# Four-layer graph network on one core: layer 2's nodes transposed by VectorE and transfers, with the surrounding products in a new order

## The chip, the cores and the metric

One core of one Trainium2 chip runs the whole kernel in one launch. The metric is the device time in microseconds (us). The kernel before took 3103.06 us, the median of three runs (3100.27 to 3104.02). Its profile below was taken on a further execution of 3099.01 us, with a span of 3097.3 us and a mean granted TensorE clock of 0.996.

Engines are named as the profile names them: PE is TensorE, PEld its weight load, DVE VectorE, ACT ScalarE, POOL GpSimd, SP SyncE (here only an issuer of transfers).

## The reference, cut to what matters

A batch of 128 graphs with 128 nodes and 256 features passes through four layers. Each is a graph layer with a residual and a layer norm. All is float32.

```python
x = _layernorm(x + L0(x))                       # attention over 512 edges
x = _layernorm(x + L1(x))                       # relu((A*A) @ x @ W1), relu((A*A) @ . @ W2), (A*A) @ . @ W3
# --- layer 2 ---
adj_0 = jnp.diag(jnp.diagonal(adj)); adj_1 = jnp.triu(adj, k=1); adj_2 = jnp.tril(adj, k=-1)
h = jnp.einsum('bjf,kfo->kbjo', x, W)           # W: 3 x 256 x 256
out = adj_0 @ h[0] + adj_1 @ h[1] + adj_2 @ h[2] + bias
x = _layernorm(x + out)
x = _layernorm(x + L3(x))                       # two products with batch norms over all rows
```

What matters here is layer 2. Its product contracts over the 256 features, so TensorE needs x with features on the partitions. Layer 1 leaves it with nodes on the partitions, so every batch element must be transposed.

## The kernel before

Four batch elements make a quad; there are 32. `iteration(k)` works on several quads at once in a software pipeline: layer 3's first product of quad a, the end of layer 1 and then layer 2 of quad c, layer 0 and the start of layer 1 of quad b = c + 1, and the scores and softmax of quads further ahead. The program order is fixed by hand; each engine runs its own instructions in that order.

Products are done in blocks with seven multiplications in place of eight (`Seven`). Three banks, y, z and x, collect them. A step that writes into y again must wait until ScalarE has copied the partial sum out (`part`):

```python
class Seven:
    def p1(self):  self.y = ps("y"); self.mm(self.y, "A11", "B11", True);  self.k1 = self.part(self.y, 0)
    def p5(self):  self.z = ps("z"); self.mm(self.z, "S1", "T1", True)
    def p2(self):  x = ps("x");      self.mm(x, "A12", "B21", True);       self.out(0, 0, x, self.k1)
    def p6(self):  self.mm(self.y, "S2", "T2", False); self.k2 = self.part(self.y, 1)
    def p7(self):  self.mm(self.y, "S3", "T3", False); self.k3 = self.part(self.y, 2); self.out(1, 1, self.z, self.k3)
    def p4(self):  self.mm(self.y, "A22", "T4", False); self.out(1, 0, self.y, None)
    def p3(self):  self.mm(self.z, "S4", "B22", False); self.out(0, 1, self.z, self.k2)
```

S1 to S4 are sums of blocks of the nodes, made by VectorE (`sums_a`). In layer 1's first product (`first_seven`, called w) `part` is a ScalarE copy, and `out` a VectorE sum followed by a ScalarE relu:

```python
def part(bank, i):
    to = room[2 + i % 2]
    nc.scalar.copy(to, bank)
    return to
def out(row, col, bank, kept_):
    h1 = temp("h1")
    if kept_ is not None:
        nc.vector.tensor_add(h1, bank, kept_)
    nc.scalar.activation(h1, bank if kept_ is None else h1, AF.Relu)
```

The third product of layer 1 and its norm, for a pair of batch elements (j = 0 or 2):

```python
def third_mix(k, j):
    po = ps("po1")
    nc.tensor.matmul(po, wt_t, s.s3[j], start=True, stop=True)
    nc.vector.tensor_add(xj, xj, po.rearrange("p (b d) -> p b d", d=D))
    s.mv = norm_stats(wk, xj)                       # two statistics, two aggregations
def third_norm(k, j):
    norm_apply(wk, xj, s.mv, norm_root(wk, s.mv))   # ScalarE root; VectorE reciprocal and scaling
    nc.gpsimd.tensor_add(s.xb[:, j:j + 2, :], xj, bias...)
```

Layer 2 works on two pairs, p = 0 and 1, each with a `Seven` (u and v). Before the first one the nodes are transposed by TensorE into PSUM and copied by ScalarE:

```python
def head(p):
    pt = ps("pt3").rearrange("p (t c n) -> p t c n", t=2, c=DC)
    for t in range(2):
        for c in range(DC):
            nc.tensor.transpose(pt[:, t, c, :], s.xr[:, 2 * p + t, c * P:(c + 1) * P], ident)
    xt = temp("x2t").rearrange("p (t c n) -> p t c n", t=2, c=DC)
    nc.scalar.copy(xt, pt)
    return xt
...
run(u.p1, u.p2, u.p5, u.p6, v.p1, v.p2, u.p7, v.p5, v.p6, u.p4, u.p3, v.p7)
```

`mix(p)` then multiplies by the triangles of the adjacency matrix, `norm` and `normed` do the layer norm. `second(k, between)` is layer 1's second product: 14 block products of 8 matmul records each; `between[i]` hangs other work, such as the rest of layer 2 and the scores of the attention (`score`, three passes of VectorE over 128x1024), behind block product i. A different quad's transposed inputs (`load_turned`, `turn`) are already made by transfers of 32x32 blocks and VectorE's transpose.

Of the kernel before, what the change touches and what calls it, by code (L numbers as in the profile page):

```python
# [8 lines left out]
F32 = mybir.dt.float32  # L9
# [17 lines left out]
def gnn_stack(ctx: ExitStack, tc: tile.TileContext, x, adj, w_qv_t, a, w_out_t, src, dst,  # L27
# [14 lines left out]
    nc = tc.nc  # L42
# [3 lines left out]
    P = 128  # L46
# [18 lines left out]
    def ps(name):  # L65
        return psum.tile([P, 512], F32, tag="ps", name=name)
# [62 lines left out]
    with ExitStack() as phase:  # L129
# [5 lines left out]
        class Seven:  # L135
# [8 lines left out]
            def __init__(self, mm, part, out):  # L144
                self.mm, self.part, self.out = mm, part, out

            def p1(self):
                self.y = ps("y")
                self.mm(self.y, "A11", "B11", True)
                self.k1 = self.part(self.y, 0)  # L150

            def p5(self):
                self.z = ps("z")
                self.mm(self.z, "S1", "T1", True)

            def p2(self):
                x = ps("x")
                self.mm(x, "A12", "B21", True)
                self.out(0, 0, x, self.k1)

# [290 lines left out]
        def adc_tile():  # L451
            return wk.tile([P, R * N], F32, tag="adc", name="adc", bufs=1)
# [120 lines left out]
        def late_sums(k):  # L573
            m2 = [quads[k].m2[:, t].rearrange("p c b n -> p c (b n)") for t in range(7)]
            nc.vector.tensor_sub(m2[T2], m2[B22], m2[T1])
            nc.vector.tensor_sub(m2[T4], m2[B21], m2[T2])

        def second_sums():

# [120 lines left out]
        def third_norm(k, j):  # L700
# [4 lines left out]
                s.xb = wk.tile([P, QB, D], F32, tag="xb", name=f"xb{k}", bufs=1)  # L705
            nc.gpsimd.tensor_add(s.xb[:, j:j + 2, :], xj, bias.unsqueeze(1).to_broadcast([P, 2, D]))  # L706

        def layer2(k, b, room=None):

            s = quads[k]
            adc = adc_tile()
            g = [wk.tile([P, 2, 3 * D], F32, tag="ms", name="g", bufs=1) if room is None else room,
                 adc[:, :6 * D].rearrange("p (t f) -> p t f", t=2)]
            sums = [adc[:, 6 * D:], None]
            half = 3 * D // 2

            def head(p):
# [7 lines that stand above are left out]
                return xt  # L727

            def products(p, xt):
                room = sums[p] if p == 0 else temp("x2s")  # L730
# [3 lines left out]
                sums_a(a, a)  # L734
                keep = {}

                def mm(bank, i, j, new):
                    nc.tensor.matmul(bank[:, :half], a[i], layer2.blocks[j], start=new, stop=True,  # L738
                                     skip_group_check=True)

                def part(bank, i):
                    if i < 2:
# [12 lines left out]
                return Seven(mm, part, out)  # L755
# [20 lines left out]
            x0 = head(0)  # L776
            yield
            u = products(0, x0)
            if b is not None:

                pm = {i: mix2(b, i) for i in (2, 0, 1)}
                x1 = head(1)
                mixed(b, 0, pm[0])
                mixed(b, 1, pm[1])
                pm[3] = mix2(b, 3)
            else:
                x1 = head(1)
            v = products(1, x1)
            if b is not None:
                mixed(b, 2, pm[2])  # L790
                mixed(b, 3, pm[3])
            run(u.p1, u.p2, u.p5, u.p6, v.p1, v.p2, u.p7, v.p5, v.p6, u.p4, u.p3, v.p7)
            pos = [ps("po2").rearrange("p (t d) -> p t d", d=D) for _ in range(2)]
            yield
            scaled(0)
            v.p4()
            yield
            v.p3()
            po = mix(0)
            scaled(1)  # L800
            yield
            mv = norm(0, po)
            yield
            po = mix(1)
            yield
            normed(0, mv)
            mv = norm(1, po)
            yield
            normed(1, mv)
# [113 lines left out]
        def iteration(k):  # L923
            a, c, b, e, g = k - 1, k, k + 1, k + 2, k + 3
            has_c, has_b, has_e, has_g = c < NQ, b < NQ, e < NQ, g < NQ
            if has_b and b > 2:
                quads[b].xr = load_x(b)
            if has_c:
                late_sums(c)
            parts = quads[a].layer2  # L930
            if not has_c:

# [17 lines left out]
            steps = softmax_parts(e) if has_e else iter(())  # L950
            if has_c:
                between = {i: [] for i in range(14)}
                for i in (0, 1, 2, 3, 5, 7):
                    between[i].append(lambda: next(parts, None))
                between[11].append(lambda: next(steps, None))
                if has_g:
                    between[9].append(lambda: turn(g))
                    between[11].append(lambda: query_sums(g))
                for i in (12, 13):
                    between[i].append(lambda: next(steps, None))  # L960
                if has_e:
                    for c_, i in enumerate((0, 2, 4)):
                        between[i].append(lambda c_=c_: score(e, c_ + 1))
                if has_b:
                    for j, i in enumerate((5, 8, 9, 10)):
                        between[i].append(lambda j=j: by_row(b, j))
                second(c, between)
# [56 lines left out]
                pass  # L1024
            if has_e:
                attention(e)
                scatter(e)
            rest = third(c, 2)
            mix1(b, 0)
            mix1(b, 2)  # L1030
            third_mix(c, 0)
            next(rest)
            w = first_seven(b)
# [12 lines left out]
            w.p3()  # L1046
            quads[c].layer2 = layer2(c, b)
            next(quads[c].layer2)
            third_norm(c, 2)
            next(quads[c].layer2)  # L1050

        def iteration_0():

            late_sums(0)
# [28 lines left out]
            mix1(1, 0)  # L1083
            next(rest)
            mix1(1, 2)
            w = first_seven(1)
            next(rest)
            w.p1()
            for _ in steps:
                pass  # L1090
            run(w.p5, w.p2)
            next(rest, None)
            attention(2)
            scatter(2)
            w.p6()
            score(3, 0)
            gather_last(3)
            w.p7()
            third_mix(0, 2)
            w.p4()  # L1100
            w.p3()
            quads[0].layer2 = layer2(0, 1)
            next(quads[0].layer2)
            third_norm(0, 2)
            next(quads[0].layer2)

        def late_loads():
            nc.sync.dma_start(w3_sb, w3.rearrange("(c p) f -> p c f", p=P))
# [562 lines left out]
```

## Time and profile before

| Part of the profile | Value |
|---|---|
| Span | 3097.3 us |
| Instructions | 39721 |
| TensorE clock granted, mean | 0.996 |
| Transposes of layer 2 on PE (L724) | 256, 273 ns each as recorded |
| Copies of them on ACT (L726) | 64, 578 ns median |
| Transposes by VectorE of xg (L336) | 56, 685 ns median |
| Data moved | 340.06 MB, mean 110 GB/s |
| Packets | 220962, of them 132704 under 512 bytes |

The busy time of an engine is an average over stages and does not by itself say what sets the end. PE records overlap, since a matmul is recorded with its whole passage: of two that follow each other, the distance of their starts is the time that PE is held. A float32 matmul appears as two records. An idle time shown in brackets names the instruction that ended the wait. Idle time of an engine counts only where PE, directly or through others, has to wait for that engine.

### The profile page before, as it was taken

How to read it: one execution, taken by the hardware profiler on the slowest of the kernel's cores; microseconds unless marked ns; L12 is line 12 of the kernel's file. 1: busy time of each engine (PE TensorE's matmuls, PEld its weight loads, DVE VectorE, ACT ScalarE, POOL GpSimd, SP SyncE). 2: the span in 40 equal slices, each digit the busy share in tenths (PEclk: the TensorE clock that was granted, in tenths of full speed). 3: DMA queues.
4: the chain of work that ended last, by engine and by line, in shares of the span. 5: the costliest groups of instructions: out<-in, count | busy, mean ns of one | idle time of the engine just before them, and what ended most of it. 6: DMA issues, size and time to landing. Idle time of an engine off the chain costs nothing. (4 is left out here: it accounts for less than half of the span.)

```text
span 3097.3 us, 39721 instructions
## 1 busy us (share of the span) xinstructions
PE 3047.4 (98%) x14576; PEld 2382.0 (77%) x14576; DVE 2311.5 (75%) x4599; ACT 1388.0 (45%) x2547; POOL 652.6 (21%) x536
## 2 busy tenths in 40 slices
PE   8899999999999999999999999999999999999987
PEld 4688888888888888888888888888888887864444
DVE  8777777777777777777777777777777776457888
ACT  3344444344444444443344444444443344326668
POOL 3311112222222121122222211111122220001135
PEclk9999999999999999999999999999999999999999
DMA  5633333334333333333344433333343331015567
GB/s 183 162 103 95 77 97 110 103 103 110 110 103 93 99 103 88 84 103 108 98 110 110 110 96 90 109 95 75 98 110 103 103 110 42 21 44 201 172 206 261
DMA packets 220962, 340.06 MB, mean 110 GB/s; under 512 B 132704, under 2 KB 155104, under 8 KB 212448
## 3 DMA queue, kind: packets, MB, share of 16 engines
q0 software_dynamic: 44688, 148.40, 19.6%
q1 hardware_dynamic: 174320, 188.19, 18.5%
q8 instruction: 116, 1.90, 0.2%
q10 hardware_dynamic: 1760, 0.92, 0.1%
q14 instruction: 78, 0.64, 0.1%
HBM read 252.00 MB, written 85.46 MB: 109 GB/s over the span
## 5 line engine op out<-in xcount | busy, mean ns | idle before, releaser
L602 PE MATMUL ph<-m,w 128*128 128x256 f32 x2048 | 473.1, 379 | 0.0
L682 PE MATMUL p<-w,h 128*128 128x256 f32 x2048 | 462.8, 379 | 0.0
L602 PEld LDWEIGHTS ph<-m,w 128*128 128x128 f32 x2048 | 386.8, 190 | 79.9 <-issue 14.8
L682 PEld LDWEIGHTS p<-w,h 128*128 128x128 f32 x2048 | 388.9, 190 | 66.4 <-issue 7.9
L358 POOL DMA_INDIRECT zs<-qd,src_idx x120 | 116.3, 969 | 1330.2 <-DMA qd<-qt 1295.8
L602 PE MATMUL ph<-m,w_s 128*128 128x256 f32 x1536 | 357.7, 379 | 0.4 <-DVE h L614 0.4
L602 PEld LDWEIGHTS ph<-m,w_s 128*128 128x128 f32 x1536 | 291.7, 190 | 53.7 <-issue 14.8
L358 POOL DMA_INDIRECT zs<-qd,dst_idx x120 | 189.6, 1580 | 339.7 <-DMA zs<-qd,src_idx 330.2
L608 ACT COPY u<-ph 128x512 f32<-128x512 f32 x128 | 74.8, 584 | 354.9 <-PE ph L602 354.9
L440 POOL DMA_INDIRECT attd<-at,att_idx x128 | 142.8, 1116 | 342.3 <-DMA attd<-at,att_idx 251.0
L113 ACT ACTIVATE ln_sd<-ln_mv,eps 128x2 f32<-128x2 f32 x192 | 55.9, 291 | 276.4 <-DVE ln_mv L108 276.3
L618 ACT ACTIVATE h<-h 128x512 f32<-128x512 f32 x192 | 121.1, 631 | 87.2 <-DVE h L614 87.2
L390 DVE SCALAR_TENSOR_TENSOR zs<-zs 128x1024 f32<-128x1024 f32 x125 | 151.3, 1210 | 7.7 <-DMA zs<-qd,dst_idx 5.1
L392 DVE TENSOR_TENSOR zs<-zs,a_bc 128x1024 f32<-128x1024 f32 x125 | 153.2, 1225 | 4.3
L393 DVE TENSOR_REDUCE scores<-zs 128x16 f32<-128x1024 f32 x125 | 152.5, 1220 | 4.3
L745 ACT COPY x2k<-y 128x384 f32<-128x384 f32 x192 | 92.0, 479 | 139.5 <-PE y L738 114.2
L106 DVE BATCH_NORM_STATS2 ln_st<-xr 128x6 f32<-128x256 f32 x384 | 144.5, 418 | 6.6
L121 DVE TENSOR_SCALAR xr<-xr,ln_mv,ln_rs 128x256 f32<-128x256 f32 x384 | 142.5, 413 | 7.0
L459 ACT COPY adc<-ad 128x512 f32<-128x512 f32 x125 | 133.0, 1066 | 7.8 <-DMA ad<-attd 7.8
L706 POOL TENSOR_TENSOR xb<-xr,bias 128x512 f32<-128x512 f32 x64 | 99.1, 1548 | 150.8 <-DVE xr L121 143.7
L559 PE MATMUL pm<-wt_t,h 128*128 128x128 f32 x1024 | 126.8, 277 | 0.0
L559 PEld LDWEIGHTS pm<-wt_t,h 128*128 128x128 f32 x1024 | 121.2, 192 | 1.4 <-issue 1.3
(359 smaller groups left out, 5990.7 us busy)
## 6 DMA issues: line engine op xcount, KB each, us to landing
ad<-attd SPq DMA_DIRECT2D x32, 1024.0 KB, 4.8
zd<-z SPq DMA_DIRECT2D x31, 1024.0 KB, 7.5
zl<-zd SPq DMA_DIRECT2D x62, 512.0 KB, 3.7
xr<-in_x_dram SPq DMA_DIRECT2D x32, 512.0 KB, 7.2
x3d<-xr SPq DMA_DIRECT2D x32, 512.0 KB, 2.6
x3l<-x3d SPq DMA_DIRECT2D x32, 512.0 KB, 4.6
out_dram<-x3l POOLq DMA_DIRECT2D x31, 512.0 KB, 5.0
qd<-qt SPq DMA_DIRECT2D x29, 512.0 KB, 2.6
```

Of the source, the lines that this page charges most:

```text
L106: nc.vector.bn_stats(st[:, i, :], r[:, i, :])
L121: nc.vector.tensor_scalar(r[:, i, :], r[:, i, :], mv[:, i, 0:1], rs[:, i:i + 1], op0=ALU.subtract, op1=ALU.mult)
L358: nc.gpsimd.indirect_dma_start(out=s.z[c], out_offset=None, in_=s.qd, in_offset=bass.IndirectOffsetOnAxis(ap=idx[:, c:c + 1], axis=0), com ...
L390: nc.vector.scalar_tensor_tensor(z, z, SLOPE, z, op0=ALU.mult, op1=ALU.max)
L392: nc.vector.tensor_mul(z3, z3, a_bc.unsqueeze(1).to_broadcast([P, QB, D]))
L393: nc.vector.reduce_sum(s.es[:, c, :], z.rearrange("p (r d) -> p r d", d=DH), axis=AX.X)
L440: nc.gpsimd.indirect_dma_start(out=ad, out_offset=bass.IndirectOffsetOnAxis(ap=att_idx[:, c:c + 1], axis=0), in_=s.at[:, c, :], in_offset= ...
L459: (copy or nc.scalar.copy)(s.adc[:, j * H:(j + 1) * H, :], s.ad.rearrange("p (s r) -> p r s", r=R)[:, j * H:(j + 1) * H, :])
L559: nc.tensor.matmul(pm[:, c // 2, c % 2, :], quads[k].h1[i, c], wt_t, start=True, stop=True)
L602: nc.tensor.matmul(bank[g][:, i].rearrange("p b n -> p (b n)"), wa[:, c, f:f + P], s.m2[:, blk_b, c].rearrange("p b n -> p (b n)"), start= ...
L618: nc.scalar.activation(h, h if src_ is None else src_, AF.Relu)
L682: nc.tensor.matmul(p3[:, t * D:(t + 1) * D], s.h2[f // 2][:, f % 2, j + t, :], w3_sb[:, f, :], start=(f == 0), stop=(f == K2 - 1))
```

## The change

The change takes the transposes of layer 2 off TensorE for 31 of the 32 quads. VectorE transposes the 32x32 blocks of two batch elements in one instruction, and 16 transfers within on-chip memory put the blocks in their places; that is done twice a quad. The result is put into two slots (T2 and T4) of the buffer m2, which layer 1's second product of the next quad will fill later. For that, the sums that fill them (`late_sums`) move into `second`. To give the transfers time, the third product of layer 1 is drawn ahead, the block products of layer 1 and layer 2 are interleaved in a new order, v's products move into `second`, the scores move to other places, and the loading of the attention weights (`load_weights`) comes after the first 16 transfers. The last quad keeps the old form.

```diff
+        def nodes_ahead(k, b):
+            s = quads[k]
+            s.g = wk.tile([P, 2, 3 * D], F32, tag="ms", name="g", bufs=1)
+            s.x2 = [quads[b].m2[:, t].rearrange("p c b n -> p (c b n)") for t in (T2, T4)]
+
+        def turn_nodes(k, p, turned):
+            s = quads[k]
+            nc.vector.transpose(turned, s.xr[:, 2 * p:2 * p + 2, :].rearrange("p b d -> p (b d)"))
+            to = s.x2[p].rearrange("p (m n) -> p m n", n=N)
+            from_ = turned.rearrange("p (m i a) -> p m i a", i=P // B, a=B)     # B = 32
+            for i in range(P // B):
+                for j in range(N // B):
+                    nc.sync.dma_start(to[i * B:(i + 1) * B, :, j * B:(j + 1) * B], from_[j * B:(j + 1) * B, :, i, :])
 ... layer2, where there is a next quad b:
+                u.p1()
+                yield
+                u.p2()
+                yield
+                g[1] = adc_tile()[:, :6 * D].rearrange("p (t f) -> p t f", t=2)
+                u.sums()
+                u.p5()
+                pm = {2: mix2(b, 2)}
+                u.p6()
+                pm[0] = mix2(b, 0)
+                pm[1] = mix2(b, 1)
                 mixed(b, 0, pm[0])
                 mixed(b, 1, pm[1])
+                u.p7()
                 pm[3] = mix2(b, 3)
                 mixed(b, 2, pm[2])
+                u.p4()
+                u.p3()
                 mixed(b, 3, pm[3])
 ...
+                yield                    # from here on in second() of the next iteration
+                v.sums(); scaled(0); po = mix(0); v.p1()
+                yield
+                mv = norm(0, po); run(v.p2, v.p5, v.p6)
+                yield
+                v.p7(); normed(0, mv)
+                yield
+                v.p4()
+                yield
+                v.p3(); scaled(1)
+                yield
+                po = mix(1)
+                yield
+                mv = norm(1, po)
+                yield
+                normed(1, mv)
 ... iteration:
-            if has_c:
-                late_sums(c)
-                for i in (0, 1, 2, 3, 5, 7):
+                between[2].append(lambda: late_sums(c, 0))
+                between[4].append(lambda: late_sums(c, 1))
+                for i in (0, 1, 2, 3, 4, 5, 6, 8):
                     between[i].append(lambda: next(parts, None))
-                    for c_, i in enumerate((0, 2, 4)):
+                    for c_, i in enumerate((2, 4, 7)):
                         between[i].append(lambda c_=c_: score(e, c_ + 1))
 ... iteration, after the first mixing products of quad b:
             third_mix(c, 0)
             next(rest)
+            third_norm(c, 0)
+            nodes_ahead(c, b)
+            turn_nodes(c, 0, quads[c].g...)
+            load_weights(e)
             w = first_seven(b)
-            third_norm(c, 0)
-            next(rest)
-            run(w.p1, w.p5, w.p2)
-            next(rest)
             score(g, 0)
             gather_last(g)
+            next(rest)
+            next(rest)
+            w.p1()
+            next(rest, None)
+            w.p5()
+            third_mix(c, 2)
+            w.p2()
+            parts = quads[c].layer2 = layer2(c, b)
             w.p6()
-            next(rest, None)
+            third_norm(c, 2)
+            turn_nodes(c, 1, kept["adc"][:, :512])
+            next(parts)
             w.p7()
-            third_mix(c, 2)
+            next(parts)
             w.p4()
             w.p3()
-            quads[c].layer2 = layer2(c, b)
-            next(quads[c].layer2)
-            third_norm(c, 2)
-            next(quads[c].layer2)
+            next(parts)
```

The first iteration is changed in the same way.

More of the change, by code (lines that the diff above doesn't have):

```diff
@@ L145, in __init__ @@
                 self.mm, self.part, self.out = mm, part, out
+            y = z = x = None
             def p1(self):
-                self.y = ps("y")
+                if self.y is None:
+                    self.y = ps("y")
                 self.mm(self.y, "A11", "B11", True)
@@ L152, in p5 @@
             def p5(self):
-                self.z = ps("z")
+                if self.z is None:
+                    self.z = ps("z")
                 self.mm(self.z, "S1", "T1", True)
             def p2(self):
-                x = ps("x")
+                x = ps("x") if self.x is None else self.x
                 self.mm(x, "A12", "B21", True)
@@ L571, in mixed, with late_sums @@
             nc.vector.tensor_sub(m2[T3], m2[B22], pm[:, 0])
-        def late_sums(k):
+        def late_sums(k, *parts):
             m2 = [quads[k].m2[:, t].rearrange("p c b n -> p c (b n)") for t in range(7)]
-            nc.vector.tensor_sub(m2[T2], m2[B22], m2[T1])
-            nc.vector.tensor_sub(m2[T4], m2[B21], m2[T2])
+            if 0 in parts:
+                nc.vector.tensor_sub(m2[T2], m2[B22], m2[T1])
+            if 1 in parts:
+                nc.vector.tensor_sub(m2[T4], m2[B21], m2[T2])
         def second_sums():
@@ L706, in third_norm @@
             nc.gpsimd.tensor_add(s.xb[:, j:j + 2, :], xj, bias.unsqueeze(1).to_broadcast([P, 2, D]))
+        def nodes_ahead(k, b):
[10 more added lines that the diff above has]
+                    nc.sync.dma_start(to[i * B:(i + 1) * B, :, j * B:(j + 1) * B], from_[j * B:(j + 1) * B, :, i, :])
         def layer2(k, b, room=None):
             s = quads[k]
[L713 to L716, printed above, removed]
+            if b is None:
+                adc = adc_tile()
+                g = [room, adc[:, :6 * D].rearrange("p (t f) -> p t f", t=2)]
+                sums = [adc[:, 6 * D:], None]
+            else:
+                g = [s.g, None]
+                both = wk.tile([P, 2, 512], F32, tag="h2", name="x2s", bufs=4)
+                sums = [both[:, p] for p in range(2)]
             half = 3 * D // 2
@@ L729, in products @@
             def products(p, xt):
-                room = sums[p] if p == 0 else temp("x2s")
+                room = sums[p] if sums[p] is not None else temp("x2s")
                 a = {f"A{t + 1}{c + 1}": xt[:, t, c, :] for t in range(2) for c in range(DC)}
@@ L733, in products @@
                     a[f"S{i + 1}"] = room[:, i * N:(i + 1) * N]
-                sums_a(a, a)
+                if b is None:
+                    sums_a(a, a)
                 keep = {}
@@ L741, in part @@
                 def part(bank, i):
-                    if i < 2:
+                    if i < 2 and i not in keep:
                         keep[i] = temp("x2k")
@@ L753, in out @@
                         nc.vector.tensor_add(to, bank[:, :half], kept_)
-                return Seven(mm, part, out)
+                seven = Seven(mm, part, out)
+                seven.sums, seven.keep = lambda: sums_a(a, a), keep
+                return seven
             def scaled(p):
@@ L774, in normed @@
                 norm_apply(wk, s.xr[:, 2 * p:2 * p + 2, :], mv, norm_root(wk, mv))
[L776 to L781, printed above, removed]
-                x1 = head(1)
+            if b is None:
+                x0 = head(0)
+                yield
+                u = products(0, x0)
+                x1 = head(1)
+                v = products(1, x1)
+                run(u.p1, u.p2, u.p5, u.p6, v.p1, v.p2, u.p7, v.p5, v.p6, u.p4, u.p3, v.p7)
+                pos = [ps("po2").rearrange("p (t d) -> p t d", d=D) for _ in range(2)]
+                yield
+                scaled(0)
+                v.p4()
+                yield
+                v.p3()
+                po = mix(0)
+                scaled(1)
+                yield
+                mv = norm(0, po)
+                yield
+                po = mix(1)
+                yield
+                normed(0, mv)
+                mv = norm(1, po)
+                yield
+                normed(1, mv)
+            else:
+                u, v = (products(p, s.x2[p].rearrange("p (t c n) -> p t c n", t=2, c=DC)) for p in range(2))
+                u.p1()
[9 more added lines that the diff above has]
+                pm[1] = mix2(b, 1)
@@ L783, in layer2 @@
                 mixed(b, 0, pm[0])
                 mixed(b, 1, pm[1])
+                u.p7()
                 pm[3] = mix2(b, 3)
[L786 to L789, printed above, removed]
                 mixed(b, 2, pm[2])
+                u.p4()
+                u.p3()
                 mixed(b, 3, pm[3])
-            run(u.p1, u.p2, u.p5, u.p6, v.p1, v.p2, u.p7, v.p5, v.p6, u.p4, u.p3, v.p7)
-            pos = [ps("po2").rearrange("p (t d) -> p t d", d=D) for _ in range(2)]
@@ L794, in layer2 @@
[L794 to L809, printed above, removed]
+                v.x, po_0 = ps("x"), ps("po2")
+                v.y, v.z, po_1 = ps("y"), ps("z"), ps("po2")
+                pos = [po.rearrange("p (t d) -> p t d", d=D) for po in (po_0, po_1)]
@@ new lines, in layer2 @@
+                for i in range(2):
+                    v.keep[i] = temp("x2k")
+                yield
+                v.sums()
+                scaled(0)
+                po = mix(0)
+                v.p1()
+                yield
+                mv = norm(0, po)
+                run(v.p2, v.p5, v.p6)
+                yield
+                v.p7()
+                normed(0, mv)
+                yield
+                v.p4()
+                yield
+                v.p3()
+                scaled(1)
@@ L810, in layer2 @@
+                yield
+                po = mix(1)
+                yield
+                mv = norm(1, po)
+                yield
+                normed(1, mv)
             nc.sync.dma_start(x3_dram[k], s.xr.rearrange("p b d -> p (b d)"))
@@ L1026, in iteration @@
                 attention(e)
-                scatter(e)
+                scatter(e, False)
             rest = third(c, 2)
@@ L1032, in iteration @@
             next(rest)
+            third_norm(c, 0)
+            nodes_ahead(c, b)
+            turn_nodes(c, 0, quads[c].g.rearrange("p t f -> p (t f)")[:, :512])
+            if has_e:
+                load_weights(e)
             w = first_seven(b)
-            third_norm(c, 0)
-            next(rest)
-            run(w.p1, w.p5, w.p2)
-            next(rest)
             if has_g:
@@ L1040, in iteration @@
                 gather_last(g)
+            next(rest)
[6 more added lines that the diff above has]
+            parts = quads[c].layer2 = layer2(c, b)
             w.p6()
-            next(rest, None)
+            third_norm(c, 2)
+            turn_nodes(c, 1, kept["adc"][:, :512])
+            next(parts)
             w.p7()
-            third_mix(c, 2)
+            next(parts)
             w.p4()
             w.p3()
-            quads[c].layer2 = layer2(c, b)
-            next(quads[c].layer2)
-            third_norm(c, 2)
-            next(quads[c].layer2)
+            next(parts)
         def iteration_0():
-            late_sums(0)
+            late_sums(0, 0, 1)
             between = {i: [] for i in range(14)}
@@ L1085, in iteration_0 @@
             mix1(1, 2)
+            nodes_ahead(0, 1)
+            turn_nodes(0, 0, quads[0].g.rearrange("p t f -> p (t f)")[:, :512])
             w = first_seven(1)
@@ L1090, in iteration_0 @@
                 pass
-            run(w.p5, w.p2)
             next(rest, None)
+            w.p5()
+            third_mix(0, 2)
+            w.p2()
             attention(2)
-            scatter(2)
+            scatter(2, False)
+            parts = quads[0].layer2 = layer2(0, 1)
             w.p6()
+            third_norm(0, 2)
+            turn_nodes(0, 1, kept["adc"][:, :512])
+            load_weights(2)
+            next(parts)
+            w.p7()
+            next(parts)
+            w.p4()
+            w.p3()
             score(3, 0)
             gather_last(3)
[L1098 to L1105, printed above, removed]
+            next(parts)
         def late_loads():
```

## The prediction

> **What bounds the kernel now.** I read the page from the top. Part 1, columns: engine, busy us, share of the span, instructions.
>
> ```profile
> PE 3047.4 (98%) x14576; PEld 2382.0 (77%) x14576; DVE 2311.5 (75%) x4599; ACT 1388.0 (45%) x2547; POOL 652.6 (21%) x536
> ```
>
> TensorE (PE) is busy almost all the time. The loop handles four batch elements (a quad) per pass. I took one pass from the middle, from the first block product of layer 1's second multiplication to the next one, and asked for its busy time. Columns: stretch, length, then busy us and instructions for PE, PEld, DVE, ACT and POOL, then granted clock, DMA share, GB/s.
>
> ```profile
> 1017.66:1102.44 84.78, 84.78 (x427) 69.83 (x426) 63.48 (x126) 36.23 (x66) 17.29 (x14) 1.00 0.37 100
> ```
>
> PE has no recorded gap in 84.78 us at full clock. Adding what its instructions need at the spacing they show when they follow each other freely gives about 84.2 us, so only some 0.6 us of a pass is hidden waiting. Work taken off PE is therefore gained in full, and any wait of PE is lost in full. Everything turns on the waits, which I read from the timeline of all engines. Columns: start us, length, engine, line, operation, tiles; in brackets the idle time before it and its releaser.
>
> ```profile
> 1082.52 0.69 DVE L539 TENSOR_TENSOR h<-x,adc 128x512 f32<-128x512 f32 x1 [2.13 <-PE x L302]
> ...
> 1083.25 0.63 ACT L540 ACTIVATE h<-h 128x512 f32<-128x512 f32 x1 [1.94 <-DVE h L539]
> ...
> 1085.04 0.59 ACT L533 COPY adc<-y 128x512 f32<-128x512 f32 x1 [1.16 <-PE y L302]
> ...
> 1087.69 0.59 ACT L533 COPY adc<-y 128x512 f32<-128x512 f32 x1 [0.28 <-PE y L302]
> ...
> 1088.42 1.03 PE L302 MATMUL y<-w_s,mx 128*128 128x256 f32 x4
> ...
> 1089.29 1.03 PE L302 MATMUL z<-w,adc 128*128 128x256 f32 x4
> ...
> 1090.16 0.60 PE L724 MATMUL pt<-ident,xr 128*128 128x128 f32 x4
> ...
> 1090.51 0.66 DVE L539 TENSOR_TENSOR h<-z,adc 128x512 f32<-128x512 f32 x1
> 1090.59 2.90 PE L559 MATMUL pm<-wt_t,h 128*128 128x128 f32 x24
> ...
> 1093.33 0.64 PE L724 MATMUL pt<-ident,xr 128*128 128x128 f32 x4
> ...
> 1093.80 1.06 PE L559 MATMUL pm<-wt_t,h 128*128 128x128 f32 x8
> ```
>
> Two things are to be seen. The eight transposes (L724) hold PE for 0.43 + 0.47 = 0.90 us a pass (1090.16 to 1090.59, 1093.33 to 1093.80). And ScalarE's copies of the bank y (L533), which free y for the next product into it, find ScalarE idle: it was waiting for PE.
>
> **What the Trainium skill says.** "TensorE: Matmul & The Clock Gate", Part 4: PE-mode transpose, says a TensorE transpose does a full 128x128 block but lands in PSUM and needs a copy; it gives about 275 ns. The trace agrees on the length (273 ns), yet four cost PE only 0.43 us, as they overlap. "VectorE: DVE Perf Modes", The three transpose paths, says VectorE turns 32x32 blocks only. So transfers must move the blocks; the existing transposes of xg (686 ns each below) likewise get blocks moved by transfers. "DMA: Bandwidth & Descriptors", Anatomy of one DMA, gives about 2.0 us of fixed cost; the small loads below land in 1.9 to 2.6 us. "PSUM — Partial Sum Buffer", Engine vs sequencer instructions, says ScalarE's and VectorE's queues are strict FIFO. The timeline shows nothing overtaking, and my case rests on that.
>
> Costs of the new parts, from the view of tile xg in that pass:
>
> ```profile
> L218 SPq DMA_DIRECT2D xg<-in_x_dram x8: 332/487/490, 1043.1 to 1046.7; - x8
> L336 DVE STREAM_TRANSPOSE xt<-xg x2: 670/686/702, 1041.8 to 1042.4; 128x512 f32<-128x512 f32 x2
> ...
> DMA to landing us min/median/max: 1.9/2.3/2.6
> ```
>
> **The change, part by part.** All 31 passes that have a next quad change; the last keeps its old form.
>
> Removed: PE 0.90 us; ScalarE two copies of 0.58 us (not bounding). Gain 0.90 us a pass, at most 31 x 0.90 = 28 us.
>
> Added: VectorE 2 x 0.69 = 1.4 us on 63.5 busy, off the path by itself. The queue of SyncE gets 32 transfers of 16 KB; 128-row ones there take 0.32 us to issue, with a gap some 0.38 us. That makes 16 x 0.38 = 6.1 us, and about 2 us more to land.
>
> First half. In the old timeline third_mix(c,0) ends on PE at 1076.21; statistics, root, scaling and transpose put the first transfer near 1080.1 and the last landing near 1080.1 + 6.1 + 2 - 0.4 = 1087.8. PE now does 12 products of `third` (5.18), p1 (0.86), four more (1.73), p5, third_mix(c,2), p2, p6 (0.86 each), so u.p1 is due at about 1087.5. Transfers are hidden but for a few tenths. The second half has slack of about 1 us on VectorE and 3 on PE.
>
> The new order costs more. I take u.p1's due time as zero.
>
> 1. **w.p7 waits for ScalarE.** VectorE now does third_mix(c,2)'s add and statistics before w.p2's sum. PE ends third_mix at -1.73; +0.20 to VectorE, +1.61 for add and statistics (1076.41 to 1078.02 in the old trace), +0.69 for the sum: 0.77. Only then can ScalarE do w.p2's relu (0.04 + 0.54), and behind it, in its queue, the copy of y after w.p6 (0.59): 1.94. With 0.14 to PE (the old trace: copy ends 1088.28, product 1088.42) w.p7 starts at 2.08. PE is free at 0.65, after u.p1. Stall 1.4 us, which also swallows a u.p1 late by up to about 1.4.
> 2. **w.p4 waits for the copy after w.p7**, with only u.p2 (0.65) between: 0.86 + 0.20 + 0.59 + 0.14 = 1.79 from w.p7's start, against 1.51. Stall 0.3, of which 0.1 was there before: 0.2.
> 3. **u.p5 waits for VectorE.** It follows w.p3 at once on PE and uses S1. On VectorE S1 stands behind w.p3's sum: 0.20 + 0.65 + 0.28 + 0.1 = 1.25 us with nothing for PE. Before, transposes and mixing products stood here.
> 4. **mix(1) waits for v.p3's sum.** From the end of product 2 of `second` PE reaches mix(1) after three products of 1.73 and three of 0.65: 7.1 us. VectorE must do, from the same end: 0.2, total 0.61, first late sum 0.70, v.p7's sum 0.47, scaling of the norm 0.84, a score 3.65, second late sum 0.65, v.p3's sum 0.56: 7.7. Stall 0.6.
>
> Sum: -0.90 + 1.4 + 0.2 + 1.25 + 0.6 = +2.55 us a pass, x 31 = +79 us, so 3182. Each stall is a difference of two sums, and a queue that stalled once has caught up elsewhere; I shade this to **3170 us**.
>
> **Rivals.**
> - (a) The order hides everything and the transposes are simply gone: 3103 - 28 = 3075 us. For it: PE is the bound and had nearly no waits; the new positions look chosen to give the transfers time. Against: points 1 and 3 need an engine to overtake its own queue.
> - (b) Transfers are the new wait: u.p1 waits on all 16. If each took 0.49 us to issue, like the 512-row loads of xg (median 487 ns), they would land near 1089.6, u.p1 would stall 2.1 us and take in point 1; the pass would then cost about 3.2 us more: 3205. Against: 128-row transfers on this queue issue in 0.32 us.
> - (c) VectorE's growing backlog becomes the bound in `second` (12.49 busy of 13.92 us from 1032.74 to 1046.66 before). I find PE reaching the score transpose and the queries' S1 just after VectorE, so I count nothing.
> - (d) Only some stalls are real, say points 3 and 4 without 1: about +1.1 a pass, 3137.
>
> **Range and chances.** Low 3105 is the gain eaten by one stall; high 3215 adds rival (b). Slower by over 2% means above 3165, or +2.0 a pass; my sum is above that, though not by far: 0.55. Faster by over 2% would need 62 us, more than twice what is removed: 0.02. The rest, 0.43, lies within, rival (a) among it.
>
> **What would show it.** PE's transposes of xr in layer 2 fall from 256 to 8. In the waits of PE and PEld: bank y of first_seven on its ScalarE copy, about 1.4 us x 31 (point 1); z of layer 2 on VectorE's x2s, about 1.2 x 31 (point 3); mix(1) on VectorE's sum into adc, 0.6 x 31 (point 4). Waits of y of layer 2 on the transfers should be under 1 us each (else rival b). I am wrong if PE again shows no gaps in a pass of some 84 us.

## The result, and the profile after

The changed kernel took **3372.88 us** against 3101.87 us for the kernel before on the same chip: 1.0875 times as long (95% interval 1.0855 to 1.0895). That is 271 us more, or 8.7 us for each of the 31 changed passes; 3170 was predicted, with 3215 as the upper end.

Part 1 of the page after answers to the line of part 1 shown before (engine, busy us, share of the span, instructions):

```profile
PE 3107.2 (92%) x14328; PEld 2392.7 (71%) x14328; DVE 2356.8 (70%) x4661; ACT 1346.3 (40%) x2485; POOL 650.1 (19%) x536
```

PE has 248 records fewer (14576 to 14328): the transposes are gone. Yet it is busy 60 us longer, and its share fell from 98% to 92%. So there are two things to look for: idle time, and the same work done more slowly. The mean granted clock of TensorE says the second too: 0.968, against 0.996 before.

The view by stretches shows both. The columns are those of the stretch shown before: stretch, length, then busy us and instructions for PE, PEld, DVE, ACT and POOL, then granted clock, DMA share, GB/s. The first line is a whole pass, the next two are parts of it.

```profile
1105.69:1199.34 93.65, 86.47 (x415) 69.97 (x414) 64.65 (x127) 34.33 (x64) 17.33 (x14) 0.96 0.38 95
1186.68:1193.42 6.74, 1.02 (x5) 0.60 (x4) 3.19 (x10) 1.30 (x3) 3.34 (x4) 0.92 0.52 137
1193.42:1199.34 5.92, 5.92 (x13) 4.01 (x13) 1.17 (x2) 1.69 (x3) 2.36 (x2) 0.52 0.96 222
```

A pass is 93.65 us instead of 84.78. In one stretch of 6.74 us PE works for 1.02 us only, and in the 5.92 us after it every record of PE runs at about half the clock. Who ended the wait is read from the timeline of the same stretch (start, length, engine, line, operation, tiles, count; in brackets the idle time before it and its releaser):

```profile
1180.24 10.28 SPq L728 DMA_DIRECT2D m<-g  x16
...
1186.68 1.03 PE L306 MATMUL y<-w_s,adc 128*128 128x256 f32 x4
...
1188.87 0.57 ACT L537 COPY adc<-y 128x512 f32<-128x512 f32 x1
...
1193.42 1.62 PE L765 MATMUL y<-l2w,m 128*128 128x384 f32 x2 [5.72 <-DMA m<-g]
...
1201.44 0.88 PE L765 MATMUL z<-l2w,x2s 128*128 128x384 f32 x2 [1.07 <-DVE x2s L185]
```

The first transfer starts at 1180.24, 4.0 us after third_mix(c,0) ends on PE (1176.24); the prediction had 3.9 (1076.21 to 1080.1). But SyncE's queue needs 10.28 us to issue the sixteen, not 6.1. u.p1 could have started near 1187.55, one product of 0.86 us after 1186.68; it starts at 1193.42, 5.9 us late. Its own two records then take 1.62 us, where they take 0.81 at full clock.

The waits of PE over the whole run (engine, bank, line, releaser; us in total, times, longest us) show that it is so in nearly every pass:

```profile
PE y L765 <- DMA m<-g: 159.4, 30, 7.5
PE z L765 <- DVE x2s L185: 40.7, 31, 4.7
PE po L793 <- DVE adc L780: 11.1, 29, 0.4
```

The second and third lines are the prediction's points 3 and 4. Points 1 and 2 are not among PE's waits: ScalarE's copy for w.p7 ended at 1189.44, while PE was still waiting for the transfers, and the steps behind u.p1 run at half the clock.

**The theory after this result:** the new order costs what the sum of the prediction says, and the rest is the sixteen transfers: their issue takes 0.64 us each, and TensorE is then slow because it had been idle. **Rivals:** the order is the main cost and the transfers only show in the same place; the slow clock is the main cost and the wait a small one; or the transfers are slow for a reason that another shape of them would remove.

### The profile page after: what moved, and what is told of

Its sections match the earlier page's. It is cut to its first block, busy times and chain, and to the rows that moved or that the text cites. A ratio compares the mean times of both kernels' runs of the same rounds, so it can differ in the third digit from the quotient of the medians.

```text
span 3372.1 us, 40643 instructions
## 1 busy us (share of the span) xinstructions
PE 3107.2 (92%) x14328; PEld 2392.7 (71%) x14328; DVE 2356.8 (70%) x4661; ACT 1346.3 (40%) x2485; POOL 650.1 (19%) x536
## 5 line engine op out<-in xcount | busy, mean ns | idle before, releaser
L765 PE MATMUL y<-l2w,m 128*128 128x384 f32 x124 | 71.9, 671 | 166.9 <-DMA m<-g 159.4
L543 DVE TENSOR_TENSOR h<-z,adc 128x512 f32<-128x512 f32 x62 | 42.9, 691 | 211.0 <-ACT adc L537 171.0
L765 PEld LDWEIGHTS y<-l2w,m 128*128 128x128 f32 x124 | 26.4, 241 | 193.3 <-issue 193.0
L563 PEld LDWEIGHTS pm<-wt_t,h 128*128 128x128 f32 x1024 | 130.3, 193 | 26.4 <-issue 2.2
```

The lines of the kernel that those rows point to most:

```text
L563: nc.tensor.matmul(pm[:, c // 2, c % 2, :], quads[k].h1[i, c], wt_t, start=True, stop=True)
```

## The experiments

Each ratio is to the kernel before on the same chip, with its 95% interval.

### One transfer in place of sixteen

All of the change stays, but one transfer of 256 KB takes the place of the sixteen. It leaves out the rearrangement of the blocks.

```diff
-            for i in range(P // B):
-                for j in range(N // B):
-                    nc.sync.dma_start(to[i * B:(i + 1) * B, :, j * B:(j + 1) * B], from_[j * B:(j + 1) * B, :, i, :])
+            nc.sync.dma_start(s.x2[p], turned)
```

> The changed kernel with each group of 16 transfers of 16 KB replaced by one of 256 KB from the same source to the same slots, in the same place of the queue. The rearrangement of the 32x32 blocks is left out, so layer 2 works on wrongly placed blocks; every other instruction and every wait stays. Theory 1 (the 16 issues at about 0.64 us each are the loss, directly and through the clock that falls in the wait): u.p1 waits no more, the clock stays at 1.0, and what is left is the new order's own waits of the prediction, -0.90 + 1.4 + 0.2 + 1.25 + 0.6 = +2.55 us a pass: 3180 us, between 3140 and 3190. Theory 2 (the new order itself costs most of the 271 us): it stays above 3300.

Measured: 3184.85 us, 1.0267 (1.0246 to 1.0287). A pass is mostly 87.4 us. From the timeline of this kernel:

```profile
1123.83 0.81 PE L763 MATMUL y<-l2w,m 128*128 128x384 f32 x2
1125.77 1.13 PE L306 MATMUL y<-w_s,adc 128*128 128x256 f32 x4 [1.14 <-ACT adc L537]
...
1127.63 1.13 PE L306 MATMUL y<-w_s,mx 128*128 128x256 f32 x4
1128.60 1.03 PE L306 MATMUL z<-w,adc 128*128 128x256 f32 x4
1130.70 0.88 PE L763 MATMUL z<-l2w,x2s 128*128 128x384 f32 x2 [1.07 <-DVE x2s L185]
```

u.p1 no longer waits, and the order's waits stand open. From u.p1 to w.p7 are 1.94 us where 0.65 would do, so point 1 costs 1.29. From w.p7 to w.p4 are 1.86 where 1.51 would do, point 2. From w.p3 to u.p5 are 2.10 where 0.86 would do, so point 3 costs 1.24. What follows: without the sixteen transfers the order alone costs 83 us, and 188 of the 271 us hang on how the transfers are made.

### Filling the wait with work

The changed kernel with 24 products of ones into the bank y ahead of u.p1. They add nothing to the result (u.p1 clears the bank) and keep TensorE from being idle.

```diff
+                u.y = ps("y")
+                for _ in range(24):
+                    nc.tensor.matmul(u.y[:, :N], ones, ones, start=True, stop=True)
                 u.p1()
```

> The changed kernel with 24 extra matmuls of a constant tile (128x128, about 0.22 us each, 5.2 us in all) into the bank y just before u.p1, that is in the 5.7 us in which TensorE waits for the transfers. They add nothing to the results. Theory 1 (the products after the wait run slowly because the granted clock fell during the wait; 5.9 us at 0.52): the clock stays near 1.0 and about 2.85 us a pass come back, 31 x 2.85 = 88 us: 3285. Theory 2 (they are slow because the transfers crowd the memory at the same time, DMA busy 0.96): no gain, 3373 or more.

Measured: 3337.33 us, 1.0758 (1.0737 to 1.0780); mean clock 0.994. From its timeline:

```profile
1176.80 5.52 PE L833 MATMUL y<-ones 128*128 128x128 f32 x48
1182.16 0.81 PE L765 MATMUL y<-l2w,m 128*128 128x384 f32 x2
```

u.p1 is back at 0.81 us: the slow clock was gone, and it was the idle time that had caused it. But only 36 us came back where 88 were expected. The stretch from u.p1 to u.p5 fell from 7.6 to 5.7 us in the mean of 23 passes, while u.p1 itself came 0.6 us later (the products don't end just when the data lands). The expectation had counted everything that ran slowly as lost. In one_transfer, with no slow clock, the same stretch takes 7.0 us, since there point 1 costs 1.3 us in it. So in the changed kernel the slow clock took the place of a wait that would have been there anyway. It is real, and it is the smaller part.

### What a transfer costs to issue

This program computes no part of the network. SyncE issues groups of sixteen transfers, between on-chip buffers and to and from DRAM, in several shapes.

```diff
+    for i, j in q:      # a, as in the kernel: 32 partitions, 4 pieces of 32 words
+        nc.sync.dma_start(blocks(a)[i * B:(i + 1) * B, :, j, :], blocks(src)[j * B:(j + 1) * B, :, i, :])
+    # then the same shape to DRAM and from DRAM (b, c); on-chip again: 32 x 128 words (d),
+    # 128 x 32 (e), 128 x 4 x 32 (f), 32 x 16 x 32 (h), 128 x 512 (k); from DRAM 32 x 16 x 32 (g)
```

> No part of the network: only groups of 16 transfers each, issued by SyncE one after another, each group waiting for the one before, so the time of one issue can be read per shape (the output is a copy of the last buffer). Groups: a on-chip 32 partitions x 4 runs of 128 bytes (as in the change), b the same from on-chip to DRAM, c the same from DRAM, d on-chip 32 x one run of 512 bytes, e on-chip 128 x one run of 128 bytes, f on-chip 128 x 4 runs of 128 bytes, g from DRAM 32 x 16 runs (as the loads of xg), h on-chip 32 x 16 runs, k on-chip 128 x one run of 2048 bytes. Theory 1 (on-chip to on-chip with 32 partitions on both sides is slow): a, d and h near 0.64 us or more, b, c, e, f, g, k near 0.35 to 0.53. Theory 2 (the number of runs per transfer sets it): a, b, c and e alike, d fastest, f, g and h slowest. Theory 3 (the issue itself is always 0.32 us and only other traffic held the queue): a near 0.35.

From the timeline of SyncE's queue (start, us from the first issue to the end of the last, transfer, count):

```profile
6.50 10.43 SPq L35 DMA_DIRECT2D a_chip32x4x<-src  x16
...
22.09 7.47 SPq L39 DMA_DIRECT2D dr<-a_chip32x4x  x16
29.67 7.49 SPq L44 DMA_DIRECT2D c_load32x4x<-dr  x16
...
74.48 10.64 SPq L67 DMA_DIRECT2D g_load32x16x<-dr  x16
...
97.58 10.37 SPq L77 DMA_DIRECT2D k_chip128x<-h_chip32x16x  x16
```

Between on-chip buffers sixteen issues take 10.1 to 10.9 us whatever the shape: one piece a partition or several, 32 partitions or 128, 16 KB or 256 KB. The kernel's small shape (32 partitions, four pieces each) to or from DRAM takes 7.5 us, 0.47 each. But DRAM at one end does not make an issue short by itself: the loads of group g, with sixteen pieces a partition, take 10.64 us, as long as the same shape on chip (10.71). Each of the three theories is wrong in part: e, f and k are as slow on chip as the shapes with 32 partitions; b and c, with as many pieces as a, are faster; and no group is near 0.35 us an issue. What all groups share is that sixteen issues in a row take 7.5 us or more, however few their bytes.

### The same blocks by way of DRAM

If the number of issues counts, fewer should help. Here one store to DRAM (where the kernel's inputs lie) and four loads take the place of sixteen transfers, with the same result as the changed kernel.

```diff
-                for j in range(N // B):
-                    nc.sync.dma_start(to[...], from_[...])           # 16, on-chip
+            nc.sync.dma_start(nd, turned)                            # 1 store to DRAM
+            for i in range(P // B):
+                nc.sync.dma_start(to[i * B:(i + 1) * B], from_[i])   # 4 loads, 32x16x32 words
```

> The changed kernel with the 16 on-chip transfers of each half replaced by one store of the turned tile to DRAM and four loads that bring the 32x32 blocks to their places; nothing is left out, the order of all else is that of the change. Theory 1 (it is the number of back-to-back transfers, 16 x 0.64 us, that makes TensorE wait): about 2.6 us for the store, 4 x 0.65 to issue and 2.6 to land is 7.8 us in place of 13; u.p1 is due 7.3 us after the first issue and waits on ScalarE's copy anyway, so the time is that of the one-transfer kernel, 3185, between 3175 and 3205. Theory 2 (small pieces are slow by themselves): above 3300.

Measured: 3204.16 us, 1.0333 (1.0313 to 1.0353), just inside what was expected. Most passes take 87.4 us, as in one_transfer; others 88 to 92. So 169 of the 188 us come back with a version that leaves nothing out.

### Only the first half

The kernel before, with its order of products, but the first pair turned by VectorE and transfers: once with the sixteen, once by way of DRAM. The second pair stays on TensorE. The load of the attention weights goes behind the first pair's transfers.

```diff
-            x0 = head(0)
+            x0 = head(0) if b is None else s.x2...      # filled by turn_nodes, called after third_norm(c, 0)
+            third_norm(c, 0)
+            turn_nodes(c, b)
             w = first_seven(b)
```

> The kernel before with only the first pair of each quad transposed by VectorE and 16 transfers, the second pair still by TensorE; the order of products is that of before, so that u.p1 comes after the second transposes and four mixing products. Theory 1 (issue time against the time at hand): first issue at about +80.2 us of the pass as in the changed kernel, last landing near +93.4, u.p1 due near +94.2: hidden, and four transposes (0.43 us) are gained: 31 x 0.43 = 13 us, 3089. Theory 2 (transfers of this kind slow other things, or the order of before has no room either): 3102 or more.

> The kernel before with the first pair of each quad transposed by VectorE and moved by one store to DRAM and four loads, the second pair by TensorE as before, nothing left out. Theory 1: with 16 transfers the data came about 0.4 to 1 us late for VectorE's sums, which cost 34 us; at 7.8 us the data is there 5 us early and the four transposes are gained: 31 x 0.43 = 13 us, 3089. Theory 2 (the loss of the run with 16 transfers came from VectorE's extra 0.7 us and the new order of its work): about 3120 to 3136 again.

Measured: 3136.04 us, 1.0108 (1.0091 to 1.0124), and 3102.98 us, 1.0004 (0.9996 to 1.0013). Both missed; 3089 was expected of both. With the sixteen, the data still comes late, in an order that gives the transfers more time: VectorE's first sum for u starts 1.75 us ahead of u.p1 in the passes without loss, and in 22 of 31 passes 0.3 to 1.7 us later than that. In eight of these the sum also takes 1.25 to 2.74 us in place of 0.28, each time beside an addition of GpSimd (xb); why is open. By way of DRAM the sum is 1.75 us ahead in nearly every pass, and there is still no gain. The timeline and the waits of first_half_dram show why:

```profile
1092.60 3.29 PE L560 MATMUL pm<-wt_t,h 128*128 128x128 f32 x24
1095.73 0.60 PE L739 MATMUL pt<-ident,xr 128*128 128x128 f32 x4
```

```profile
PEld pm L560 <- ACT h L541: 17.1, 62, 0.4
```

The 24 records of the mixing products hold PE for 3.13 us, start to start; before they held it for 2.74. They read h, which ScalarE's relus make after w.p4 and w.p3: two waits of some 0.28 us a pass in the weight loads, where the kernel before shows none. There the four transposes stood between w.p3 and these products and covered the wait. Taking 0.43 us of transposes away opened 0.39 us of waiting; from w.p3 to u.p1 are 5.36 us where 5.40 were before.

### Mending the order

By way of DRAM, with the four waits of the order undone: w.p2 before third_mix(2), the second half turned after w.p7, the sums of u before u.p2, the first score earlier. The second version also moves the load of the attention weights behind the second half's transfers; the third has the mended order with the sixteen on-chip transfers again; the fourth gives v one more block product of time, which moves its sums and two scores to later places.

```diff
             w.p5()
+            w.p2()
             third_mix(c, 2)
-            w.p2()
             ...
-            turn_nodes(c, 1, kept["adc"][:, :512])
             next(parts)
             w.p7()
+            turn_nodes(c, 1, kept["adc"][:, :512])
+            load_weights(e)             # mended2: here, not after the first half's transfers
```

> As the kernel with DRAM in both halves, with the four waits of the prediction mended: w.p2 before third_mix(c,2) (so ScalarE's relu and copy are not held by the norm's statistics), the transpose of the second half after w.p7's sum, u's sums ahead of w.p3's sum on VectorE, and the first score at block product 0 in place of 2 (so v.p3's sum is in time for mix(1)). Theory 1 (waits 1 to 4 are caused by those positions): of the +2.67 us a pass of the one-transfer kernel about 0.3 to 0.6 us of waits remain against the 0.90 gained: 3102 - 31 x 0.45 = 3088, between 3075 and 3110. Theory 2 (the waits come back elsewhere since VectorE has no room): 3140 or more.

> As the kernel mended before, with the 1 MB load of the attention weights moved behind the second half's store and four loads in SyncE's queue; nothing is left out. In that kernel the four waits of the order were gone, but the second half's store was issued 1.9 us after the weights' load and landed 6.7 us later, and TensorE waited 2.3 us for it. Theory 1 (it waits behind the weights in the transfer queue): the store lands in about 2 us, the wait goes, and a pass takes 84.0 to 84.3 us against 84.8: 3102 - 31 x 0.6 = 3083, between 3075 and 3095. Theory 2 (GpSimd's gather of 512 KB is what it waits for): about 3150 to 3170 again.

> The same mended order with the 16 on-chip transfers of the change in each half in place of the store and four loads; nothing is left out. Theory 1 (16 issues of 0.64 us make u.p1 wait, whatever the order, and the clock falls in the wait): u.p1 due 7.3 us after the first issue, data 13.2 us after it, 5.9 us of wait and about 2 us of slow clock on 84.1: 3102 + 31 x 7.2 = 3325, between 3300 and 3345. Theory 2 (the waits of the order and those of the transfers overlap, so that mending the order gives nothing back): 3370.

> As the kernel mended a second time (3103 us, passes of 84.3 us with others of 85 to 86 where v.p1 waited up to 1.5 us for the second half's loads), with v's products one block product of layer 1 later: v.p1 and v.p2 after block product 1, p5 and p6 after 2, and so on, the second late sum after 5, the scores after 0, 5 and 8. Nothing is left out. Theory 1 (v.p1 lacks about 1.5 us): it now comes 1.7 us later, nearly all passes take 84.3 us, 3102 - 31 x 0.45 = 3088, between 3080 and 3098. Theory 2 (VectorE has no room left in this stretch, so its later sums hold TensorE instead): 3103 or more.

Measured for mended: 3170.47 us, 1.0221 (1.0207 to 1.0235), where 3088 was expected. The waits of points 3 and 4 are gone and those of points 1 and 2 are small, but a new one has come. From SyncE's queue, then from PE, in the timeline of mended:

```profile
1107.50 0.33 SPq L454 DMA_DIRECT2D ad<-attd  x1
1109.38 0.33 SPq L726 DMA_DIRECT2D nd<-adc  x1
1116.11 3.23 SPq L730 DMA_DIRECT2D m<-nd  x4
```

```profile
1122.44 1.62 PE L767 MATMUL y<-l2w,m 128*128 128x384 f32 x2 [2.25 <-DMA m<-nd]
```

The load of the attention weights, 1 MB, is issued 1.9 us ahead of the second half's store. The loads that need that store are issued only 6.7 us after it, and v.p1 waits. After 2.25 us of idle TensorE its records again take 1.62 us. With the weights loaded later (mended2) the time is 3103.17 us, 1.0000 (0.9991 to 1.0008). The line of the same wait, in mended and then in mended2:

```profile
PE y L767 <- DMA m<-nd: 56.7, 27, 4.0
```

```profile
PE y L767 <- DMA m<-nd: 9.6, 11, 1.5
```

So the collision with the 1 MB load was the cause in mended. mended2 should still have taken 3083. Its best passes take 84.3 us, 0.5 less than before and not 0.9. The rest is what is left of points 1 and 2: the weights of w.p7 and of w.p4 are loaded as soon as ScalarE's copy of y ends.

```profile
1088.22 0.73 PEld L307 LDWEIGHTS y<-w_s,adc 128*128 128x128 f32 x4 [0.65 <-ACT adc L538]
...
1090.08 0.73 PEld L307 LDWEIGHTS y<-w_s,mx 128*128 128x128 f32 x4 [0.70 <-ACT adc L538]
```

From u.p1 to w.p7 are 0.84 us and from u.p2 to w.p4 0.89, where 0.65 would do (u.p1 to w.p7 in filled, where the copy is long done): together 0.43 us. About a third of the passes take 85 to 86 us, because the second half's data is late.

The mended order with the sixteen transfers (mended_16) takes 3345.5 us, 1.0782 (1.0760 to 1.0803), just above the expected 3300 to 3345. It is 242 us above mended2, which differs only in how the blocks are moved. This excludes the first rival: the transfers, not the order, are the bulk. It is also only 27 us below the changed kernel: under the wait for the transfers most of the order's 83 us is hidden, so the two costs are no fixed shares of the 271.

mended3 takes 3109.68 us, 1.0028 (1.0016 to 1.0039), where 3088 was expected. From the waits of PE in mended3:

```profile
PE y L307 <- ACT m L324: 9.6, 28, 0.3
```

The wait for the transfers is down to a single one of 1.0 us, and most passes take a steady 85.1 us. But VectorE, with its work moved, is late at the end of layer 1's second product. In the timeline of one pass ScalarE sits idle 2.53 us before VectorE's sum comes and its last relu there can start, in mended2 1.78. Behind that relu in ScalarE's queue is the copy of layer 0's bank y, and PE waits 0.34 us for it; from layer 0's first product to the product of attention and values (py) are 11.07 us, in mended2 10.46. That is rival (c) of the prediction, in a small form. No version here beats the kernel before.

### The queue by itself

Two more programs without any part of the network. In the first the groups ran into each other, since their order in the program was not kept; the second fixed the order.

```diff
+        # a: 12 on-chip transfers, each reading what the one before wrote
+        # b, e: 16 on-chip from SyncE; c: 8 from SyncE and 8 from ScalarE; d: one store to DRAM, 4 loads
```

> No part of the network: groups of on-chip transfers of 16 KB, each group waiting for the one before (the output is a copy of the last buffer). a: 12, each reading what the one before wrote; b and f: 16 back to back from SyncE; c: 8 from SyncE and 8 from ScalarE in turn; d: 8 from SyncE and 8 from GpSimd; e: one store to DRAM and four loads. Theory 1 (0.64 us is the pace of one issuing queue, an issue by itself takes 0.32): a 0.32 us each, b and f about 10.3 us in all, c about half, d between, e under 8 us until the last lands. Theory 2 (the pace is that of the transfers themselves, shared by all queues): c as long as b; a 0.32 or 0.6.

> No part of the network: as the kernel queues, but with the program order kept, since there the groups ran into each other. a: 12 on-chip transfers of 16 KB, each reading what the one before wrote; b and e: 16 back to back from SyncE; c: 8 from SyncE and 8 from ScalarE in turn; d: one store to DRAM and four loads. Theory 1 (an on-chip transfer holds its issuer 0.5 to 0.6 us even alone): a 0.5 to 0.6 us each. Theory 2 (only when back to back): a 0.32. Whether the pace is one queue's own: c about 5.5 us in all if it is, about 10.5 if it is shared. d: last load issued about 4.7 us after the store.

From SyncE's queue in the timeline of queues_in_order:

```profile
25.78 10.33 SPq L33 DMA_DIRECT2D b_sp<-a_chain  x16
...
43.30 0.34 SPq L49 DMA_DIRECT2D nd<-c_sp_act  x1
45.40 2.61 SPq L53 DMA_DIRECT2D d_store_back<-nd  x4
```

The store and the four loads are issued in 4.7 us (43.30 to 48.01), the sixteen in 10.3. A transfer that waits for the one before takes 0.51 us to issue, against 0.60 in a row, so most of the cost is there without another issue just ahead of it.

Of the group shared by two queues, ScalarE's first transfers came early and with waits of their own, so the group as a whole says little. But there is a stretch in which both queues issue, almost without a pause:

```profile
36.06 4.09 ACTq L33 DMA_DIRECT2D c_sp_act<-b_sp  x6
36.21 4.23 SPq L33 DMA_DIRECT2D c_sp_act<-b_sp  x6
```

Twelve issues take 4.4 us here, 0.36 each; SyncE's own take 0.70 each, against 0.65 alone. So the pace is nearly one queue's own. Whether the kernel would gain from it was not tried; ScalarE would spend some 0.6 us on each issue. The first program told nothing of it.

## Why the prediction was wrong, point by point

**The step that failed** is the duration of the transfers: "16 x 0.38 = 6.1 us, and about 2 us more to land", and from it "hidden but for a few tenths". The 0.32 us behind the 0.38 came from transfers of 128 rows to and from DRAM. The kernel before had none between on-chip buffers, so its profile held no row for them; the nearest row was taken as if it were the same thing. The view of the attention weights' load before, and of the sixteen after (lengths of an issue in ns, smallest, median, largest):

```profile
L449 SPq DMA_DIRECT2D ad<-attd x32: 319/320/350, 60.1 to 2606.8; - x32
```

```profile
L728 SPq DMA_DIRECT2D m<-g x496: 585/599/1618, 144.5 to 2962.0; - x166
```

With the gap it is 0.64 us. The term was short by two things: sixteen of the kernel's small shape take 7.5 us even with DRAM at one end, as against 6.1, and 10.4 on chip (shapes). In the kernel the term 6.1 was 10.3, the landing with the start of the product 2.9, and so u.p1 starts 13.2 us after the first issue (1180.24 to 1193.42) where the prediction had the last landing at 7.7. Rival (b) named the mechanism, but had 0.49 us, the median issue of the loads of xg. It was argued away with the same wrong row.

**A term that was missing** is the clock. The prediction counted a wait at its own length. A long wait also makes TensorE slow after it: 0.50 of full clock from about 1192.4 to 1199.1 in the view by single microseconds. The Trainium skill, "TensorE: Matmul & The Clock Gate", Part 1: The HAM clock gate, says that the clock is halved after an idle window of about 3.4 us and comes back after about as long at work. The halving agrees, 0.50; but in mended it came 2.1 us after the last product, within an idle time of 2.25 us. It then held for 3.3 us of work there, about as the page says, and for 5.7 in the changed kernel. Its cost was smaller than it looked (filled).

**What held.** The order's costs, as one_transfer and after show them beside the prediction:

| Step | Predicted, us a pass | Measured |
|---|---|---|
| Transposes removed | -0.90 | gone, 248 records fewer |
| 1: w.p7 on ScalarE's copy | 1.4 | 1.29 |
| 2: w.p4 on the next copy | 0.2 | 0.35, of which 0.1 before |
| 3: u.p5 on S1 | 1.25 (its terms add up to 1.23) | 1.24 |
| 4: mix(1) on v.p3's sum | 0.6 | 0.55 (2.28 start to start, less 1.73) |
| Whole kernel with these alone | 3182 | 3184.85 |

So the sum of the prediction was right for the order alone, and shading it to 3170 was not. That the whole agrees within 3 us is in part luck: the measured terms add up to 2.43 us a pass, and the kernel lost 2.67. Rival (a) is excluded for this order by the waits of points 3 and 4. Rival (d) is excluded by one_transfer, where all four are present.

**The account of a pass**, from means over 23 passes in the middle of each run: 84.8 us before; 87.6 in one_transfer, so +2.8 for the order; then from one_transfer to the changed kernel +5.6 from third_mix(c,2) to u.p1 (2.66 to 8.24), +0.6 from u.p1 to u.p5 (6.98 to 7.57), and nothing in all the rest: 93.8. The late u.p1 hides point 1, and the slow clock gives it back.

**What stays open**: why an issue between on-chip buffers takes about 0.2 us longer than one of the same shape with DRAM at one end (10.43 against 7.47 us for sixteen); whether the kernel would gain from issuing half of the transfers from a second queue; and whether an order exists in which VectorE and the transfers both have room, as none of those tried did.

## What to carry to other kernels

When a change brings a kind of transfer that the profile does not hold, with other memories at its ends, measure its issue by itself before counting on it, and multiply by the number of transfers: the queue's pace, not the bytes, set the time here. Before taking work off the busiest engine, ask which wait that work was covering; here 0.43 us of transposes covered 0.39 us. A wait of some microseconds on TensorE can cost more than its length, since what follows may run at half the clock (here after 2.25 and 5.72 us), unless it would have waited there anyway.

## What the runs showed of the hardware that was not expected

- Sixteen transfers between on-chip buffers from one queue took 10.1 to 10.9 us to issue, for 16 KB and 256 KB, 32 and 128 partitions alike. With DRAM at one end the kernel's small shape took 7.5 us, loads of sixteen pieces a partition 10.64, and a single store to DRAM 0.34 us.
- Two queues hardly slowed each other: SyncE and ScalarE together issued twelve on-chip transfers in 4.4 us, SyncE's at 0.70 us each against 0.65 alone.
- One store to DRAM and four loads back were faster than sixteen transfers that never left the chip: 4.7 against 10.3 us of issue, and 3204 against 3373 us for the kernel.
- TensorE ran at 0.50 of its clock after 2.25 us of idling in mended and after 5.72 us in the changed kernel; with the idle time filled, the records were back at full length for full clock (0.81 us).
